# Softmax statistics settled once per node block, sums by source over 72 columns, and one load for edge features, in a two-layer graph kernel on Trainium2

## The chip, the cores and the metric

The kernel runs on one core of one Trainium2 chip. The core has five engines with instruction queues of their own, each worked off in order: PE (TensorE, matmuls; its weight loads are listed apart as PEld), DVE (VectorE), ACT (ScalarE), POOL (GpSimd) and SP (SyncE, which here only issues DMAs). They meet through semaphores alone. The metric is the device time of one execution in microseconds. Before the change it is 4238.74 us, the median of three runs (4227.38 to 4244.78).

## The reference, cut to what matters

6250 nodes with 128 features, 100,000 edges `src -> dst`, sorted by `dst`. Two graph layers, each with a residual and a layer norm. H = 8 heads of D = 16.

```python
# layer 0: attention; the softmax runs over the edges of one src
q, k, v = (x @ W.T + b for Wq, Wk, Wv)                   # each (N, H, D)
scores  = sum(q[src] * k[dst], -1) / sqrt(16) + edge_attr_8
seg_max = segment_max(scores, src)
ex      = exp(scores - seg_max[src])
weights = ex / segment_sum(ex, src)[src]
x = layernorm(x + segment_sum(v[src] * weights, dst) @ Wo.T + bo)
# layer 1: edge MLP, summed by src, then a node MLP
h   = silu(concat[x[src], x[dst], edge_attr_2] @ eW1 + eb1)
agg = segment_sum(silu(h @ eW2 + eb2), src)
x = layernorm(x + silu(concat[x, agg] @ nW1 + nb1) @ nW2 + nb2)
```

(The three projections are written as one line.) Three things are sums or maxima over all edges of one source node: `seg_max`, the sum of `ex`, and `agg`. The change touches all three.

## The kernel before

**Order of the edges.** The edges come sorted by `dst`. The kernel first puts them into order of `src`, in two regions: region 0 ("near") holds the edges with `dst` below 256, region 1 ("far") the others. A chunk is 16 tiles of 128 edges, 2048 edges; the near region has 9 chunks (`AC`), the far one 40 (`BC`). Each sorted edge is one row of the DRAM arrays `xs[r]`. Since the edges are in order of `src`, the edges of a few tiles touch a short run of node numbers. So a gather by `src` is a matmul: a one-hot matrix (`oh`, made by DVE by comparing a row of node offsets with the partition number) times a *window* of 128 consecutive rows of a table. A window serves `WT[r]` tiles: 2 near, 4 far, so 8 windows to a near chunk and 4 to a far one. The first node of each window is a number in a register, read at run time from `s0i`.

**Tables.** `q3_tab`, `k3_tab` and `v3_tab` in DRAM hold the projections of all nodes, each float32 value as a sum of three bfloat16 parts, 3 x 128 values to a row. `near_tab` in DRAM holds, for each node, the running maximum and sum (16 values) that the near edges gave. `stat_r` in SBUF (96 partitions x all nodes) takes the maxima and sums of the far edges: each of two slots for an edge run's maximum and sum has three bfloat16 parts, 96 rows.

**Stages of the traced execution.** Until about 1552 us: sorting, projections and `near_scores` (the scores and statistics of the near region). From 1552 to 2954: the *softmax stage*, the middle loop of `fast` (L909 on), over the far chunks with the near ones put between. To 3117: the messages, which the softmax stage scatters into `xmsg` by order of `dst`, are summed by `dst` (L1110). To 3172: output projection and first layer norm. From there to the end: the *edge layer* (`loads_of`, `pre_of`, `second`, `total`, `layer`; L1192 on).

**The softmax stage.** A far chunk passes these steps, each in quarters of a chunk:

- *fetch* (L511): SP loads the edge rows `st` and four windows `qw` of the q table, two buffers each.
- *turn* (L519): PE transposes columns of `st`; ACT writes node offsets to `slo_row` in DRAM and SP reads them back spread over all partitions; ACT writes the parts of the edge features to `ef_rows`.
- *score* (L578): DVE makes the one-hot `oht`; PE gathers q (`qv`, L587), DVE multiplies by k and reduces (`pr`, L590).
- *soft* (L598): scans along the edges give each run of equal `src` its maximum and its sum of exponentials.
- *stat* (L619): DVE makes `soh`, a one-hot of the last edge of each run against the 128 nodes of the window (L640); PE multiplies it with the values `v96` (L657); DVE adds the result into `stat_r` at the window's register address (L663).
- *merge* (L934): joins the statistics for the windows of this chunk. First quarter: SP loads the windows of `near_tab` into `z` and of `v3_tab` into `vw`, DVE copies the windows of `stat_r` into `tmp` (L949). Second: PE transposes `tmp` (L954) and DVE reduces the parts into `z` (L955). Third: `pooled` (L668) joins the slots into one maximum and one sum, then the reciprocal, then three bfloat16 parts `lw` (`split3`, L111 to L115). Fourth: PE spreads `lw` to the edges with the one-hot (L968), and DVE, ACT and DVE make the weights `wt` (L971 on). The same code joins the near chunks, which need all far chunks that reach their nodes.
- *message* (L990): PE gathers v (L979), DVE multiplies by `wt` (L981), and POOL scatters the rows into `xmsg`, one indirect DMA for each tile of 128 edges (L126).

**What sets the order.** A plan gives each step and quarter a due time: chunk number minus a lag of the step (fetch 6, turn 5, score 4, soft 3, stat 2.25, merge 0.9, message 0). `run` works off the plan in order of due times, and runs first what a step needs: `merge` of chunk c needs `stat` of chunk c+1, since the next chunk can still add to its last nodes; and `held` makes a step wait until an earlier chunk has given back a buffer (`score` of chunk c needs all messages of c-6). The compiler's scheduler may move instructions from there.

**The edge layer.** For each far step of four tiles, POOL gathers the rows of `b_tab` for `dst` (L118), PE transposes them into `pre` (L1217), adds the part of the edge features (`eft`, three loads per chunk, L1195 to L1197) and of the `src` nodes (`aw`), ACT applies SiLU; PE multiplies with `w2` (`po`), ACT applies SiLU to give `fe`; in `total`, DVE makes the one-hot `ohf` (128 columns), PE multiplies it in float32 with `fe` as the weights (`ps`, L1255), and DVE adds the 128 columns into `agg2` (L1259).

**Two branches.** The program has a fast branch, described here, and a general one. Tests on the data (`counts_fit`, `tell_path`) choose: no near or far count may leave an even spread by more than `SLACK`, and windows may not be wider than they are assumed to be.

Of the kernel before, what the change touches and what calls it, by code (L numbers as in the profile page):

```python
# [32 lines left out]
WT = (2, 4)  # L33
PER_BLOCK = (377.5, 1671.0)
SLACK = (512.0, 1024.0)
# [17 lines left out]
def tile_gnn(  # L53
# [28 lines left out]
    q3_tab, k3_tab, v3_tab, a3_tab = (dram.tile([NW, 3 * F], BF16, name=f"{n}3_tab") for n in "qkva")  # L82
    b_tab = dram.tile([NP, F], F32, name="b_tab")
    ka_tab = dram.tile([NW, 3 * F], BF16, name="ka_tab")
    near_tab = dram.tile([NW, 16], F32, name="near_tab")
# [183 lines left out]
    def rows_of_keys(r):  # L269
# [8 lines left out]
        if r == 0:  # L278
            nc.gpsimd.memset(none, -1.0)
            zero = ks.tile([P, 3 * F], BF16, name="zero")  # L280
            nc.gpsimd.memset(zero, 0.0)
            for tab in (k3_tab, q3_tab, v3_tab, a3_tab):
                nc.sync.dma_start(tab[NP:NW, :], zero)
            rows_of_keys.none = none
# [32 lines left out]
        over = ks.tile([p, g, P], F32, name=f"over{r}")  # L317
# [63 lines left out]
    def counts_fit():  # L381
# [6 lines left out]
        half = kp.tile([P, 2], F32, name="half")  # L388
        nc.vector.tensor_single_scalar(half[:, 1:2], iota_p, float(P // 2), ALU.is_ge)
        nc.vector.tensor_scalar(half[:, 0:1], half[:, 1:2], -1.0, 1.0, ALU.mult, ALU.add)  # L390
        sums = bank()[:, :NB]
        nc.tensor.matmul(sums[:2, :], half, cnts[1], start=True, stop=True)
        nc.vector.tensor_reduce(b[:2, 2:3], sums[:2, :], AX.X, ALU.min)
        nc.vector.tensor_single_scalar(b[:2, 2:3], b[:2, 2:3], float(4 * P), ALU.is_lt)
# [17 lines left out]
    def project_qv():  # L412
# [8 lines left out]
        nc.scalar.mul(bqv[:, 0], bqv[:, 0], D ** -0.5)  # L421
        for j0 in range(0, NB, 2):
# [12 lines left out]
            for a in range(3):  # L435
# [5 lines left out]
                for i, tab in enumerate((q3_tab, v3_tab)):  # L441
                    nc.sync.dma_start(
                        tab[j0 * P:(j0 + n) * P, a * F:(a + 1) * F].rearrange("(j p) f -> p j f", p=P),
# [36 lines left out]
    def scorer(r, sp, bank_q, bank_x, deep, dsti=None):  # L480

        c0, n = REG[r]
        nw = UC // WT[r]
# [4 lines left out]
        v96 = [sp.tile([P, UC, 96], BF16, name=f"v96_{i}", bufs=1) for i in range(2)]  # L488
# [19 lines left out]
        def window(tab, c, name, bufs):  # L508
            t = sp.tile([P, nw, 3, F], BF16, name=name, bufs=bufs)
# [14 lines left out]
        def turn(c, q):  # L524
# [32 lines left out]
            else:  # L557
# [11 lines left out]
                else:  # L569
                    nc.scalar.copy(dsti[:, c * UC:(c + 1) * UC], st[:, :, 1])  # L570
                    w["at"] = sp.tile([P, UC], I32, name="at", bufs=8)
# [7 lines left out]
        def score(c, q):  # L579
            w = works[c]  # L580
            if q == 0:
                w["oh"] = hot_of(w["row"], "oht", deep["oh"])
                w["dot"] = sp.tile([P, UC, H], F32, name="dot", bufs=8) if r else dota[:, c]
# [35 lines left out]
        def stat(c, q):  # L619
# [3 lines left out]
            v = v96[c % 2]  # L623
# [4 lines left out]
            if q == 0:  # L628
# [10 lines left out]
                w["soh"] = sp.tile([P, 4, P, 4], BF16, name="soh", bufs=deep["soh"])  # L639
# [1341 lines left out]
```

## Time and profile before

| | us |
|---|---|
| median of three runs | 4238.74 |
| lowest, highest | 4227.38, 4244.78 |
| the profiled execution | 4211.11 |
| its span (first to last instruction) | 4209.2 |
| PE busy in the span | 2643.5 (63%) |
| POOL | 2156.6 (51%) |
| PE weight loads | 2030.1 (48%) |
| DVE | 1994.6 (47%) |
| ACT | 861.8 (20%) |
| mean granted clock of TensorE | 0.713 of full speed |
| moved by DMA | 523.75 MB, mean 124 GB/s |

The span counts 65,902 instructions. Busy times of engines lie beside each other and don't add to the span. No engine is busy two thirds of it, so the whole says less than the stages do. The granted clock is between 0.5 and 0.8 in most slices until about 2900 us and 0.9 or more afterwards[...].

In the listings, a group of instructions is shown as: line, engine, operation, output <- input, sizes, number | busy us, mean ns of one | idle time of the engine just before these instructions, and what ended it ("PE x L957": a semaphore of PE from the write of `x` at line 957; "remote": a semaphore whose setter the trace doesn't name; "issue": nothing that is shown). An idle time belongs to the instruction that came after it, and all that stands behind it in the same queue has waited as well.

### The profile page before, as it was taken

The page shows a single profiled execution, that of the slowest core. Times are in us where ns is not written, and L with a number is a line of the kernel's source. Part 1 is how long each engine was busy: PE and PEld are TensorE (multiplying, and loading weights), DVE is VectorE, ACT ScalarE, POOL GpSimd, SP SyncE. Part 2 cuts the span into 40 slices and gives each one's busy share as a digit, 9 for nine tenths or more (in the row PEclk, how much of TensorE's full clock was granted, in tenths as well). Part 3 has the DMA queues.
Part 4 walks back from the last instruction along what each step waited for, and adds up shares of the span by engine and source line. Part 5 has one row for each costly group of instructions (what it writes and reads, how often), then busy time and mean ns, then how long its engine had stood idle before and what let it go on. Part 6 is the DMA issues. An engine that isn't in the chain of part 4 may idle for free. (4 is left out here: it accounts for less than half of the span.)

```text
span 4209.2 us, 65902 instructions
## 1 busy us (share of the span) xinstructions
PE 2643.5 (63%) x22552; PEld 2030.1 (48%) x22552; DVE 1994.6 (47%) x6056; ACT 861.8 (20%) x2688; POOL 2156.6 (51%) x2119
## 2 busy tenths in 40 slices
PE   6546674444444225555655666565895999898988
PEld 4444443333333224444544555454883666665655
DVE  6655335454545525555555556554892222222232
ACT  2222232122222111111111111110022222222222
POOL 3455544555555551445445444556216666666663
PEclk8555555566555556666676777576897899999999
DMA  5433545444543315434434344431754333333341
GB/s 180 130 118 103 143 138 168 139 151 132 167 130 100 110 60 142 135 109 133 122 113 127 114 120 117 138 98 50 281 197 128 109 100 98 99 110 98 101 124 46
DMA packets 492378, 523.75 MB, mean 124 GB/s; under 512 B 155562, under 2 KB 417117, under 8 KB 486912
## 3 DMA queue, kind: packets, MB, share of 16 engines
q1 hardware_dynamic: 399150, 345.09, 28.3%
q0 software_dynamic: 66048, 140.62, 10.9%
q10 hardware_dynamic: 26834, 33.73, 2.5%
q8 instruction: 180, 2.95, 0.3%
q14 instruction: 166, 1.36, 0.1%
HBM read 391.11 MB, written 128.06 MB: 123 GB/s over the span
## 5 line engine op out<-in xcount | busy, mean ns | idle before, releaser
L126 POOL DMA_INDIRECT xs<-stg,posi x784 | 803.9, 1025 | 766.1 <-ACT cs L777 337.0
L126 POOL DMA_INDIRECT xmsg<-msg,at x640 | 648.7, 1014 | 722.1 <-issue 409.4
L118 POOL DMA_INDIRECT bt<-b_tab,dsti x640 | 640.5, 1001 | 333.4 <-issue 165.4
L778 PE MATMUL base<-hi,lo 128*128 128x49 bf16 x784 | 169.6, 216 | 547.3 <-ACT cs L777 333.5
L780 PEld LDWEIGHTS <-hit 128*128 128x128 bf16 x2352 | 145.7, 116 | 546.5 <-issue 531.0
L1259 DVE TENSOR_TENSOR stat_r<-stat_r,ps 128x128 f32 x232 | 66.3, 286 | 645.7 <-PE ps L1255 223.4
L787 PE MATMUL kx<-kw,ohd 128*128 128x128 bf16 x2352 | 265.5, 284 | 97.0 <-issue 56.9
L762 DVE TENSOR_SCALAR_CACHE_REDUCE junk<-sk,meta 128x127 bf16<-128x127 int16 x784 | 298.1, 435 | 11.4 <-DMA sk<-skew 4.8
L777 ACT CAST cs<-base 128x49 bf16<-128x49 f32 x784 | 160.7, 205 | 638.3 <-remote 286.4
L787 PEld LDWEIGHTS <-ohd 128*128 128x128 bf16 x2352 | 213.9, 131 | 136.1 <-issue 129.3
L587 PEld LDWEIGHTS <-oht 128*128 128x128 bf16 x2352 | 219.3, 134 | 124.3 <-issue 63.8
L1255 PE MATMUL ps<-ohf,fe 128*128 128x128 f32 x1568 | 231.4, 292 | 52.1 <-issue 28.5
L587 PE MATMUL qv<-qw,oht 128*128 128x128 bf16 x1920 | 200.5, 287 | 97.7 <-DVE oht L576 36.3
L1240 PE MATMUL po<-w_sb,ht 128*128 128x128 f32 x1568 | 245.6, 301 | 18.7 <-issue 9.4
L1255 PEld LDWEIGHTS ps<-ohf,fe 128*128 128x128 f32 x1568 | 208.8, 205 | 62.0 <-issue 33.9
L1240 PEld LDWEIGHTS po<-w_sb,ht 128*128 128x128 f32 x1568 | 205.2, 203 | 66.8 <-issue 49.4
L979 PE MATMUL qv<-vw,oht 128*128 128x128 bf16 x1920 | 188.5, 257 | 74.2 <-DVE pr L590 34.0
L1232 ACT ACTIVATE ht<-pre 128x512 f32<-128x512 f32 x196 | 116.9, 597 | 493.1 <-PE pre L1228 199.6
L979 PEld LDWEIGHTS <-oht 128*128 128x128 bf16 x1920 | 152.9, 117 | 122.6 <-issue 92.3
L223 DVE TENSOR_TENSOR lo<-iota_e,lo_c 128x2048 bf16<-128x2048 bf16 x98 | 119.0, 1215 | 150.6 <-remote 80.2
L780 PE MATMUL look<-st_b,hit 128*128 128x49 bf16 x1568 | 164.3, 211 | 27.1 <-DVE sel L794 17.0
L1228 PE MATMUL pre<-oht,aw 128*128 128x512 bf16 (+1 forms) x696 | 171.9, 365 | 12.8 <-issue 12.4
(303 smaller groups left out, 5228.8 us busy)
## 6 DMA issues: line engine op xcount, KB each, us to landing
st<-xs SPq DMA_DIRECT2D x49, 1128.0 KB
srow<-slo_row SPq DMA_DIRECT2D x98, 512.0 KB
lob<-lob_row SPq DMA_DIRECT2D x49, 512.0 KB
drow<-dlo_row SPq DMA_DIRECT2D x49, 512.0 KB
sk<-skew SPq DMA_DIRECT2D x49, 508.0 KB
qw<-q_tab SPq DMA_DIRECT2D x232, 96.0 KB
vw<-v_tab SPq DMA_DIRECT2D x232, 96.0 KB
aw<-a_tab SPq DMA_DIRECT2D x232, 96.0 KB
```

The lines of the kernel that those rows point to most:

```text
L118: nc.gpsimd.indirect_dma_start(out=dst, out_offset=None, in_=table, in_offset=bass.IndirectOffsetOnAxis(ap=idx, axis=0))
L126: apart(nc.gpsimd.indirect_dma_start(out=table, out_offset=bass.IndirectOffsetOnAxis(ap=idx, axis=0), in_=src, in_offset=None), group)
L587: nc.tensor.matmul(qe[:, i, :], w["oh"][:, 4 * q + i, :], w["qw"][:, (4 * q + i) // WT[r], k, :], start=(k == 0), stop=(k == 2))
L762: nc.vector.tensor_scalar(junk, w["sk"][:, :, j], meta[:, c * UC + j, 0:1], 0.0, ALU.is_equal, ALU.add, accum_out=w["rank"][:, j:j + 1])
L777: nc.scalar.copy(cs, base)
L778: nc.tensor.matmul(base, lo, hi, start=False, stop=False, skip_group_check=True)
L780: nc.tensor.matmul(w["look"][:, j - 8 * h, :], w["hit"][:, j, :], tab, start=(i == 0), stop=(i == 2))
L787: nc.tensor.matmul(kx[:, i, :], w["ohd"][:, 4 * q + i, :], w["kw"][:, q, a, :], start=(a == 0), stop=(a == 2))
L979: nc.tensor.matmul(ve[:, i, :], w["oh"][:, 4 * q + i, :], w["vw"][:, (4 * q + i) // WT[r], k, :], start=(k == 0), stop=(k == 2))
L1228: nc.tensor.matmul(pre[:, i * wt:(i + 1) * wt, :], w["aw"][:, 4 // wt * q + i, k, :], w["oh"][:, 4 * q + i * wt:4 * q + (i + 1) * wt, :], ...
L1240: nc.tensor.matmul(po[:, i, :], ht[:, i, :], cw["w2"], start=False, stop=(i == 3))
L1255: nc.tensor.matmul(ps[:, i // WT[r], :], fe_[:, i, :], oh[:, i, :], start=(i % WT[r] == 0), stop=((i + 1) % WT[r] == 0))
```

## The change

1. **`merge` becomes `settle`, once for each block of nodes.** A block is 128 nodes, 49 in all. `settle(b)` transposes one block of `stat_r` straight from its place (no `tmp`), joins it with the near part, which stays in SBUF (`near_o`) instead of `near_tab`, makes maximum and reciprocal of the sum, splits them into three parts, and stores these into `v3_tab`, whose rows are widened from 3 x 128 to 3 x 144 values (`VW`). It runs when the last far chunk that can reach the block (`holds`) has been through *stat*. The step *load* (far) or *nfetch* (near) then loads windows of `v3_tab`, 144 columns to a part, that bring v and the statistics together; *weigh* spreads the last 16 columns to the edges as the fourth quarter of `merge` did.
2. **New lags and buffers.** fetch 8.5, turn 7.5, score 6.5, soft 5.5, stat 4.75, load 1.5, weigh 0.7, message 0. Eight buffers of the one-hot instead of six, twelve of `dot` and of `at` instead of eight; the holds of `turn` and `score` go to twelve and eight chunks back, and `load` needs the messages of three chunks back.
3. **72 columns for far sums by `src`.** `soh` with L657 and L663 in *stat*, and `ohf`, `ps` and their adds in the edge layer take the first 72 columns of a window instead of 128 (`WN`). `counts_fit` gets a test that this suffices.
4. **`eft` by one DMA** whose source repeats six rows three times, instead of three DMAs.
5. **Tighter `SLACK`**, 384 and 750 instead of 512 and 1024, and, in the general branch, two buffers of a tile instead of four. In the first stage, three stores put zeros into the new columns of `v3_tab`.

```diff
+WN = (P, 72)
-SLACK = (512.0, 1024.0)
+SLACK = (384.0, 750.0)
+VW = F + 16
...
+    v3_tab = dram.tile([NW, 3 * VW], BF16, name="v3_tab")
-    near_tab = dram.tile([NW, 16], F32, name="near_tab")
...
+        for a in range(3):
+            nc.sync.dma_start(v3_tab[:NP, a * VW + F:(a + 1) * VW].rearrange("(j p) f -> p j f", p=P),
+                              none.to_broadcast([P, NB, VW - F]))
...
-                w["soh"] = sp.tile([P, 4, P, 4], BF16, name="soh", bufs=deep["soh"])
+                w["soh"] = sp.tile([P, 4, wn, 4], BF16, name="soh", bufs=deep["soh"])
...
-                        to = sums_of["src"][:96, bass.ds(rg[i], P)]
-                        nc.vector.tensor_add(to, to, y[:96, (i - i0) * P:(i - i0 + 1) * P])
+                        to = sums_of["src"][:96, bass.ds(rg[i], wn)]
+                        nc.vector.tensor_add(to, to, y[:96, (i - i0) * wn:(i - i0 + 1) * wn])
...
+            def settle(b, q):
+
+                x = bank_x()[:, :96]
+                nc.tensor.transpose(x, sums_of["src"][:96, b * P:(b + 1) * P], ident[:96, :96])
+                z = sp.tile([P, 1, 3, 16], F32, name="z")
+                nc.vector.tensor_reduce(z[:, 0, 0:2].rearrange("p a v -> p (a v)"),
+                                        x.rearrange("p (k v) -> p v k", v=32), AX.X, ALU.add)
+                nc.scalar.copy(z[:, 0, 2], sums_of["near"][:, b])
+                o = sp.tile([P, 1, 16], F32, name="o")
+                pooled(o, z, sp, 1, 3)
+                nc.vector.tensor_scalar_max(o[:, :, 8:16], o[:, :, 8:16], 0.5)
+                nc.vector.reciprocal(o[:, :, 8:16], o[:, :, 8:16])
+                o3 = sp.tile([P, 3, 16], BF16, name="o3")
+                split3([o3[:, k, :] for k in range(3)], o[:, 0], sp, "orest")
+                nc.scalar.dma_start(v3_tab[b * P:(b + 1) * P, :].rearrange("p (k f) -> p k f", k=3)[:, :, F:], o3)
+
+            def weigh(r, w):
+
+                x = bank_x()[:, :256].rearrange("p (t v) -> p t v", v=16)
+                for t in range(UC):
+                    for k in range(3):
+                        nc.tensor.matmul(x[:, t, :], w["oh"][:, t, :], w["vw"][:, t // WT[r], k, F:],
+                                         start=(k == 0), stop=(k == 2))
...
+            def far_load(c, q):
+                works[c]["vw"] = s["window"](v3_tab, c, "vw1", 3, VW)
...
+            steps = {"fetch": (s["fetch"], 1, 8.5), "turn": (s["turn"], 3, 7.5), "score": (s["score"], 4, 6.5),
+                     "soft": (s["soft"], 2, 5.5), "stat": (s["stat"], 4, 4.75), "load": (far_load, 1, 1.5),
+                     "weigh": (far_weigh, 1, 0.7), "message": (far_message, 4, 0.0)}
...
+            held = {"fetch": (("score", 2),), "turn": (("score", 2), ("message", 12)),
+                    "score": (("message", 8),), "load": (("message", 3),)}
...
-                for i in range(3):
-                    nc.sync.dma_start(w["eft"][6 * i:6 * i + 6], ef_rows[r][:, c * UC * P:(c + 1) * UC * P])
+                row = ef_rows[r][0:1, :]
+                nc.sync.dma_start(w["eft"], bass.AP(tensor=row.tensor, offset=row.offset + c * UC * P,
+                                                    ap=[[0, 3], [REG[r][1] * UC * P, 6], [1, UC * P]]))
...
-                oh = el.tile([P, 4, P], F32, name="ohf", bufs=3)
+                oh = el.tile([P, 4, P], F32, name="ohf", bufs=3)[:, :, :wn]
...
-                ps = elq.tile([F, 2, P], F32, name="ps")
+                ps = elq.tile([F, 2, P], F32, name="ps")[:, :, :wn]
```

## The prediction, made before the result was known

> **What bounds the kernel now.** I read the busy times by stage first, since one share of the whole says little here (columns: stretch; its length, then busy time and count for PE, PEld, DVE, ACT, POOL; granted TensorE clock; DMA share; GB/s):
>
> ```profile
> 1552.00:2954.00 1402.00, 791.38 (x8346) 661.75 (x8346) 750.89 (x2153) 209.54 (x837) 672.12 (x660) 0.67 0.40 115
> 2954.00:3117.00 163.00, 149.12 (x1285) 147.70 (x1285) 143.52 (x321) 0.40 (x1) 24.43 (x14) 0.95 0.79 278
> ...
> 3172.00:4209.00 1037.00, 896.39 (x5229) 597.92 (x5229) 268.34 (x666) 241.68 (x414) 642.53 (x643) 0.90 0.35 100
> ```
>
> Two of these stages are touched. In the softmax stage (1552 to 2954) no engine is busy more than 56%, and the clock is 0.67: five in-order queues stand and wait for each other. In the edge layer (from 3172) PE is busy 86% at clock 0.90, and that is the bound; POOL comes next with 640 gathers of 1.001 us and 0.30 us of issue before each, 836 us.
>
> Who waits in the softmax stage is told by the groups of that stretch, with the idle time before them:
>
> ```profile
> L949 DVE COPY tmp<-stat_r 96x128 f32 x232 | 37.6, 231 | 4.4 <-issue 4.2
> ...
> L955 DVE TENSOR_REDUCE z<-x 128x128 f32<-128x384 f32 x58 | 31.4, 551 | 111.1 <-remote 76.2 <-PE x L954 12.6 <-issue 8.9
> ...
> L640 DVE TENSOR_TENSOR soh<-iota_e,last 128x2048 bf16<-128x2048 bf16 x40 | 48.6, 1216 | 0.0
> L663 DVE TENSOR_TENSOR stat_r<-stat_r,x 96x128 f32 x160 | 43.9, 274 | 24.4 <-PE x L657 15.7 <-PE qv L587 5.5 <-PE x L968 1.5
> ...
> L113 DVE TENSOR_TENSOR lr<-po,lw 128x64 f32<-128x64 f32 (+1 forms) x49 | 11.5, 234 | 72.2 <-ACT lw L111 37.1 <-issue 26.4 <-ACT sr L537 7.9
> ...
> L971 DVE TENSOR_TENSOR wt<-dot,x 128x128 f32<-128x128 f32 x40 | 11.4, 286 | 100.0 <-PE x L968 56.2 <-remote 15.8 <-PE x L1020 11.3
> ```
>
> To be seen: DVE, the engine that all others feed, stands 111 us before the merge's reduction, 72 us before its split and 100 us before the weights (29 more on the near form). Its queue is in order, so scores and messages behind these lines stand as well.
>
> **The change, part by part.** All sums are against the profiled execution: span 4209.2, its own time 4211.1 us. The median of the runs is 4238.7, 0.65% more; I add that at the end.
>
> *Merge becomes settle.* DVE's merge rows, L949, L955, the six of `pooled` (10.8, 12.9, 13.2, 12.8, 13.2, 13.3), L960 13.0, L961 18.7, L113 11.5 and L115 11.2, sum to 199.6 us. A settle does one block: one reduction of 96 elements (273 ns at L679's 96) and ten operations of 16 to 48 elements (between L529's 170 ns at 16 and L113's 234 at 64; I take 190), so 2.2 us; 49 of them are 106. DVE loses 94 us, its copies and their register loads wholly. PE loses 183 of 232 transposes at the 183 ns of L954's weight load, 33 us. SP loses 232 loads of `near_tab` (POOL and DMA gain nothing by it: 29,696 packets of 64 B at 10 ns over 16 engines are 19 us, spent again on wider rows of v and on 49 stores). ACT gains 49 copies and 49 DMA issues, some 0.55 us each, 27 us, beside 85% idle.
>
> *72 columns in `stat`.* `soh` is 1216 ns for 2048 columns; 56/128 of it, 40 times, is 21 us of DVE. L663's adds lose 56 columns at 1.03 ns (L1259's 286 ns at 128 against L1251's 682 at 512): 58 ns x160, 9 us. PE's 640 matmuls of L657 have weights of 96 columns, which need 96/128 of today's pitch of 107 ns (x16 in 1.83 us); they fall to that, not to 72/128: 17 us.
>
> *Waits.* Counted in instructions of all engines in the program as built (about 525 to a chunk), the weights of a chunk follow the merge's copies by about 200 today; after the change they follow the transposes of the last block that they need by 480 to 1250. So the chain reduce, Exp, split no longer ends in the same half chunk in which it began. I let half of the waits at L955 and L113 go (110 and 72, so 91) and a quarter of those at L971 (129, so 32): 123. Bounds: 0, if other waits take the place at once (pr at L590 stands 146 us already, for PE); 311, if all go.
>
> *How much of the work lies on the path.* DVE's 124 us and PE's 50 partly lie beside each other and beside the waits on PE. The chain of waits passes through PE and DVE by turns in this stage, so I take 60% of DVE's part, 74. Sum of gains in the stage: 197.
>
> *What the stage pays.* (a) Deeper lags: 20 quarters of scores stand before the first message where 12 did, and 27 messages behind the last one where 17 did. Ten messages are 40 scatters at 1.013+0.30 us, 53 us of POOL; the last stretch, 2826 to 2954, has POOL busy 74 of 128, so most fits in. I take 20; ends 0 and 53. (b) A new road through DRAM: settle's store waits on ACT for earlier loads of `v3_tab` to land (the table is read at register addresses, so every store is ordered behind every load), and `load` on SP waits for the store. The nearest row is `slo_row`: from the issue of its store to the issue of its load 1.4 to 9 us, median 2.7. Behind the waiting load on SP stand `qw` and `st` of a later chunk, and PE's turn waits for `st` (58.7 us today); behind the store on ACT stand the casts of `stat`. The load is followed by its first use within 26 to 100 instructions, 2 to 6 us. Today's loads of z stand as close (21 to 200) and cost DVE 12 us in all; I take 15. Ends 0 and 7 us per chunk, 280.
>
> *Edge layer, 72 columns.* Here a rule and a row weigh against the change. Both sides of a matmul are timed in this view (ns: minimum/median/maximum):
>
> ```profile
> L1255 PE MATMUL ps<-ohf,fe x1567: 269/275/582, 3199.7 to 4194.9; 128*128 128x128 f32 x196
> L1255 PEld LDWEIGHTS ps<-ohf,fe x1566: 186/192/338, 3199.7 to 4194.8; 128*128 128x128 f32 x196
> ```
>
> Each f32 matmul is two records. In order of time eight records stand in 1.06 us, a pitch of 112 ns, and every record has a weight load of its own. Matmul rule of the Trainium skill ("TensorE: Matmul & The Clock Gate", Back-to-back issue gap): streamed columns / 2.4 + 2.5. For two passes of 72 columns that is 63 ns; 160 steps x 8 x 49 is 62 us. Load rule of the same page (LDWEIGHTS): columns / 1.2, which is 107 ns for the 128 columns of `fe` whatever the moving side does, and its fast load is not given to f32. The trace sides with the second: the weight load is 192 ns for f32 in two passes, 142 for one pass (L1217), 98 for bf16 (L1228), so a pass of 128 columns is about 50 ns, two 100; and the first record of a run of eight takes 1.16 us with its load exposed against 1.06 us. With a load of about 104 ns to each record the pitch can fall only from 112 to about 107: 160 x 8 x 5 is 6 us. I take 5; ends 0 and 62. DVE's rows there shrink, but DVE is 26% busy and waits for PE.
>
> *One load for `eft`.* SP issues 98 DMAs fewer (0.33 us each), but SP stands over 500 us at this line for buffers. Only the first chunks gain, where PE stood 10 us for `eft`: 5 us.
>
> *First stage.* Three stores of zeros add 18,816 packets of 32 B; the 5120 of `skew` passed in 3.2 us, so 12 us of DMA, long before anything reads them; 13 stores of `near_tab` go. 0, ends -12 and +15, since the built order shifts a little. The longer test in `counts_fit` runs beside POOL's scatters. The tighter SLACK only moves `layer` earlier.
>
> Sum: -197+20+15-5-5 = -172; 4211-172 = 4039; times 4238.7/4211.1, **4066 us**, 4.1% less.
>
> **Rivals.** *A, nothing much comes free* (0.15): the stage's pace is set by `st` and `qw`, held in two buffers each, with a fetch that waits for a score two chunks back; this loop isn't touched. For it: the waits on `st` (99 us on ACT, 59 on PE) and SP's at L512, over 450 us. Against it: DVE's longest waits are in the merge. Gain 0 to 60: 4180 to 4240. *B, the load through DRAM takes the merge's place* (0.15): at PE's first weigh matmul of each chunk, behind SP's queue. If store, load and landing stand open by 7 us in each of 40 chunks, that is 280 against the 197 gained, and with (a) the time is 4211+280-197+20-10 = 4304, with the factor 4332. It decides from some 4.5 us per chunk on; below, the kernel is still faster. *C, all waits go and the matmul rule holds* (0.07): -74-311-62, with nothing paid, 3764 us, times the factor 3789; half way to it from the forecast is 3930. *D, the other branch is taken*, since the conditions are tighter: computed from the inputs, sorted far edges leave the even spread by at most 199 against 750, near ones by 109 against 384, and 512 edges span 43 nodes, under 72. Excluded.
>
> **Numbers.** The forecast with a gain of 60 to 260 (3980 to 4180) has 0.63, A 0.15, B 0.15, C 0.07. The range 3950 to 4245 holds forecast, A and a little of B and C: 0.8. Half a per cent, 21 us, is about what this measurement tells from no change: faster 0.77 (forecast, C and half of A), same 0.07, slower 0.16.
>
> **What would show it.** The softmax stage should end at about 1240 us length instead of 1402; DVE's waits before the weights' row and before the split should shrink, DVE's busy time there be near 627; `ps` records should keep a pitch of 107 to 112 ns with 72 columns. Wrong would be: PE idle before the weigh matmuls on DMA of `vw` (B), the same wait total under the names `pr` and `st` (A), a pitch near 63 (C).

## The result, and the profile after

The changed kernel takes 4273.65 us (median of 5 runs, 4268.63 to 4293.96), the kernel before 4238.74 (median of 5, 4221.04 to 4245.91): ratio 1.0099, 95% interval 1.0071 to 1.0126. It is 1% slower; 4066 us was forecast. The profiled execution takes 4268.63 us, its span 4266.8.

The busy times by stage, as for before (stretch; its length, then busy time and count for PE, PEld, DVE, ACT, POOL; granted clock; DMA share; GB/s), of the kernel after:

```profile
0.00:1586.50 1586.50, 766.97 (x7452) 591.17 (x7452) 781.98 (x2716) 377.97 (x1359) 791.06 (x782) 0.58 0.45 130
1586.50:2979.00 1392.50, 723.43 (x8163) 596.00 (x8163) 621.77 (x1913) 206.11 (x886) 657.33 (x659) 0.66 0.41 117
2979.00:3147.00 168.00, 147.81 (x1281) 146.34 (x1282) 145.03 (x320) 0.41 (x1) 24.88 (x14) 0.93 0.77 270
...
3203.00:4266.00 1063.00, 913.16 (x5228) 605.62 (x5228) 223.31 (x663) 241.21 (x413) 627.18 (x644) 0.87 0.34 97
```

The work that was to go is gone: in the second row DVE is busy 622 us (751 before, about 627 forecast) and PE 723 (791 before, some 741 forecast). The stage is 1393 us long all the same, against 1402. So DVE stands 770 us of it where it stood 651. The groups with idle time, of the kernel after in that stage (time in the group, mean ns | idle before it and what ended that):

```profile
L608 DVE TENSOR_TENSOR pr<-qv,st 128x512 f32<-128x512 f32 x160 | 108.1, 683 | 133.2 <-PE x L972 48.1 <-remote 42.1 <-PE qv L605 33.5
...
L972 PE MATMUL x<-vw,oht 128*128 128x16 bf16 x1920 | 89.1, 174 | 128.0 <-issue 116.7 <-DMA vw<-v_tab 11.1
...
L972 PE MATMUL x<-vw,noh 128*128 128x16 bf16 x432 | 28.8, 176 | 59.3 <-issue 44.4 <-DMA vw<-v_tab 14.8
...
L956 DVE TENSOR_REDUCE z<-x 128x32 f32<-128x96 f32 x49 | 11.5, 251 | 80.2 <-remote 74.9 <-PE x L954 2.6 <-PE tp L573 1.7
...
L115 DVE TENSOR_TENSOR orest<-o,o 128x16 f32<-128x16 f32 x49 | 8.1, 168 | 7.8 <-ACT o L113 7.8
...
L975 DVE TENSOR_TENSOR wt<-dot,x 128x128 f32<-128x128 f32 x40 | 11.5, 287 | 196.6 <-PE x L972 78.4 <-remote 39.3 <-PE qv L983 37.9
```

and the same matmuls of *weigh* in the kernel before, where they belonged to `merge`:

```profile
L968 PE MATMUL x<-lw,oht 128*128 128x16 bf16 x1920 | 77.2, 173 | 88.9 <-issue 51.2 <-ACT lw L111 24.9 <-ACT sr L537 6.0
...
L968 PE MATMUL x<-lw,noh 128*128 128x16 bf16 x432 | 19.0, 172 | 19.3 <-issue 18.3 <-ACT lw L111 0.7 <-DVE lw L115 0.2
```

The wait before the split fell from 72 to 8 us (L115 now). That before the reduction fell from 111 to 80, with 49 reductions in place of 58; its greater part is "remote" in both kernels (76 and 75 us). That before the weights doubled, from 100 to 197, and 78 us of it are put down to the *weigh* matmuls of PE (L972), as are 48 of the 133 us before the scores' product (L608). PE itself stands 128 + 59 us before these matmuls, against 89 + 19 before, and of the 187 us only 26 are put down to the load of `vw`. The rest is "issue": the engine waited for nothing that the trace shows.

Cut at the first and the last product of v and weights, and at the first instruction of each later stage, the two profiled executions compare so (us):

| | first stage | softmax: lead | messages | tail | sum by `dst` | node stage | edge layer | span |
|---|---|---|---|---|---|---|---|---|
| before | 1551.9 | 96.1 | 1298.4 | 8.4 | 161.6 | 66.6 | 1026.2 | 4209.2 |
| after | 1586.4 | 111.2 | 1252.2 | 29.4 | 167.6 | 62.4 | 1057.5 | 4266.8 |
| difference | +34.5 | +15.1 | -46.2 | +21.0 | +6.0 | -4.2 | +31.3 | +57.6 |

(Of the 57.6 us some 20 are the spread of executions: the profiled one of before, 4211.11, was faster than all five timed ones; the medians differ by 35.) By one profile each, the stretch of messages gained 46 us. Lead and tail took 36 back, and the first stage and the edge layer, for which no change and a gain of 10 us had been forecast, grew by 66.

### The profile page after: what moved, and what is told of

Read it like the earlier page. It is cut to its first block, busy times and chain, and to the rows that moved or that the text cites. A ratio compares the mean times of both kernels' runs of the same rounds, so it can differ in the third digit from the quotient of the medians.

```text
span 4266.8 us, 64192 instructions
## 1 busy us (share of the span) xinstructions
PE 2596.0 (61%) x22370; PEld 1974.6 (46%) x22370; DVE 1826.1 (43%) x5819; ACT 859.1 (20%) x2737; POOL 2127.4 (50%) x2120
## 5 line engine op out<-in xcount | busy, mean ns | idle before, releaser
L128 POOL DMA_INDIRECT xs<-stg,posi x784 | 802.9, 1024 | 800.0 <-ACT cs L793 380.7
L128 POOL DMA_INDIRECT xmsg<-msg,at x640 | 635.0, 992 | 728.9 <-DVE msg L986 351.9
L120 POOL DMA_INDIRECT bt<-b_tab,dsti x640 | 623.8, 975 | 378.3 <-issue 163.6
L1281 DVE TENSOR_TENSOR stat_r<-stat_r,ps 128x72 f32 (+1 forms) x232 | 57.1, 246 | 728.3 <-PE ps L1277 277.1
L1262 PE MATMUL po<-w_sb,ht 128*128 128x128 f32 x1568 | 255.4, 308 | 23.3 <-issue 14.6
L1277 PE MATMUL ps<-ohf,fe 128*128 128x72 f32 (+1 forms) x1568 | 224.6, 289 | 60.8 <-issue 45.5
L605 PEld LDWEIGHTS <-oht 128*128 128x128 bf16 x2352 | 216.6, 133 | 96.8 <-issue 69.1
L605 PE MATMUL qv<-qw,oht 128*128 128x128 bf16 x1920 | 211.6, 289 | 71.5 <-issue 48.6
L983 PE MATMUL qv<-vw,oht 128*128 128x128 bf16 x1920 | 174.8, 242 | 56.0 <-issue 36.2
L1131 PE MATMUL ps<-ohd,mt 128*128 128x128 f32 x1280 | 147.7, 279 | 56.9 <-DMA mt<-xmsg 53.7
```

What stands on the lines that cost most here:

```text
L120: nc.gpsimd.indirect_dma_start(out=dst, out_offset=None, in_=table, in_offset=bass.IndirectOffsetOnAxis(ap=idx, axis=0))
L128: apart(nc.gpsimd.indirect_dma_start(out=table, out_offset=bass.IndirectOffsetOnAxis(ap=idx, axis=0), in_=src, in_offset=None), group)
L605: nc.tensor.matmul(qe[:, i, :], w["oh"][:, 4 * q + i, :], w["qw"][:, (4 * q + i) // WT[r], k, :], start=(k == 0), stop=(k == 2))
L983: nc.tensor.matmul(ve[:, i, :], w["oh"][:, 4 * q + i, :], w["vw"][:, (4 * q + i) // WT[r], k, :F], start=(k == 0), stop=(k == 2))
L1262: nc.tensor.matmul(po[:, i, :], ht[:, i, :], cw["w2"], start=False, stop=(i == 3))
L1277: nc.tensor.matmul(ps[:, i // WT[r], :], fe_[:, i, :], oh[:, i, :], start=(i % WT[r] == 0), stop=((i + 1) % WT[r] == 0))
```

## The experiments

**Two sorts of chips.** The executions fell on several chips, each beside executions of the kernel before on the same one. On four chips before took 3243 to 3249 us (medians of 19 to 39 runs); on the chip of the result 4239, and on one more 4299 (11 runs). Same program, same data. I call them quick and slow chips below. Times can't be compared across the two sorts; what differs between them is the key to this case. A second profile of the kernel before, on a quick chip, shows where the 1000 us are:

> The kernel before, a second profile, to see how far the stages move from one execution to the next: I expect each stage within 15 us of the first profile (1552, 1402, 163, 55, 1037), and the stretches in which PE, DVE, ACT and SP advance by one instruction in 0.7 us to sum to 60 to 120 us again.

```profile
0.00:1114.00 1114.00, 711.70 (x7449) 561.90 (x7451) 777.83 (x2713) 371.41 (x1359) 801.23 (x763) 0.66 0.62 184
1114.00:2176.00 1062.00, 705.92 (x8346) 605.53 (x8346) 745.01 (x2155) 211.67 (x837) 691.38 (x678) 0.75 0.53 153
2176.00:2339.00 163.00, 149.87 (x1287) 148.44 (x1288) 142.13 (x320) 0.41 (x1) 24.07 (x14) 0.94 0.80 278
...
2395.00:3241.00 846.00, 805.10 (x5132) 558.84 (x5229) 271.02 (x665) 248.72 (x412) 625.57 (x643) 0.98 0.43 122
```

It took 3243.6 us, far outside the 15 us per stage that I had expected, and the hold-ups in steps of 0.7 us, of which a piece is shown further below, are not in it. Against the rows of the first profile, the sum by `dst` (163 us, third row) is the same. The first stage lost 438 us of 1552, the softmax stage 340 of 1402, the edge layer 191 of 1037, with nearly the same busy times of POOL and DVE. These three are the stages in which POOL issues indirect DMAs (784 + 640 scatters, 640 gathers). The three waits that the prediction took for those of `merge` (before reduction, split and weights) are 31, 21 and 35 + 7 us in this profile, 95 in all, where the first one had 312.

**The parts of the change, on quick chips.** *Settle alone*: the changed kernel with

```diff
-WN = (P, 72)
+WN = (P, P)
...
-                nc.sync.dma_start(w["eft"], bass.AP(tensor=row.tensor, offset=row.offset + c * UC * P,
-                                                    ap=[[0, 3], [REG[r][1] * UC * P, 6], [1, UC * P]]))
+                for i in range(3):
+                    nc.sync.dma_start(w["eft"][6 * i:6 * i + 6], ef_rows[r][:, c * UC * P:(c + 1) * UC * P])
```

> The changed kernel with 128 columns again in stat and in the edge layer and with three loads of eft: settle, the wide rows of v and the new lags alone. Theory 1 (the softmax stage gained nothing because of settle and the road around it): the softmax stage stays near the 1392 us of the changed kernel, at 1390 to 1430, and the first stage stays some 30 us longer than before. Theory 2 (72 columns or the single load cost what settle gains): the softmax stage falls to 1300 or less. For the edge layer: if 72 columns or the eft load made it 26 us longer, it is back at 1037 here; if it varies from execution to execution, it can be anywhere from 1030 to 1065.

> The changed kernel with 128 columns everywhere and three loads of eft, once more. Where before takes about 4240 to 4300 us: Theory 1 (the edits of the edge layer lengthened it): edge layer 1025 to 1045 here; Theory 2 (a reason outside it): 1055 or more. First stage 20 us or more longer than that of the kernels with the old first stage, by either. Softmax stage 5 to 30 us shorter than before by either. Where before takes about 3250 us: 3220 to 3230 in all, as in the first run of it.

Ratio to before 0.993 (0.9914 to 0.9947), and on a second quick chip 0.9919 (0.9903 to 0.9936). Softmax stage 1021 and 1020 us against 1062: on these chips settle, with its lags, gains 41 us there. The first stage takes 1127 and 1129, against 1111 to 1119 in six profiles with the old first stage. Neither theory's size was right, since both had the slow chip's stages in mind.

*The edge layer's edits*, each alone in the kernel before, then together, then the changed kernel without them:

```diff
-                oh = el.tile([P, 4, P], F32, name="ohf", bufs=3)
+                oh = el.tile([P, 4, P], F32, name="ohf", bufs=3)[:, :, :wn]
...
-                ps = elq.tile([F, 2, P], F32, name="ps")
+                ps = elq.tile([F, 2, P], F32, name="ps")[:, :, :wn]
```

> The kernel before with 72 columns in the edge layer alone (ohf, ps and their adds). Theory 1 (fewer streamed columns leave the matmul bound by its weight load and the granted clock falls a little): edge layer 1050 to 1065 us at a clock of 0.85 to 0.88, the whole run 10 to 25 us slower. Theory 2 (as predicted, load-bound and otherwise neutral): edge layer 1027 to 1037 us, whole run within 10 us of before. Theory 3 (the matmul rule): 975 us.

> The kernel before with the single load of eft alone. Theory 1 (as predicted): edge layer 2 to 8 us shorter than 1037, nothing elsewhere. Theory 2 (one DMA of 18 rows lands later than three of 6, and PE waits for it at the first steps of each chunk): edge layer 10 to 30 us longer, with PE idle before L1224 on DMA of eft.

> The kernel before with the two edits of the edge layer alone: 72 columns in ohf, ps and their adds, and the single load of eft. On a chip where before takes about 4240 to 4300 us: Theory 1 (these two edits lengthened the edge layer, which took 1058 to 1089 us in the changed kernel against 1026 to 1038): 1060 us or more here, clock there at 0.88 or less. Theory 2 (the edge layer is longer for a reason outside it): 1025 to 1040. Where before takes about 3250 us: 835 to 840 by either.

> The kernel before with the two edits of the edge layer, once more, since the first run of it fell on a chip where before takes 3243 us and showed 837 us by either theory. Where before takes about 4240 to 4300 us: Theory 1 (these edits lengthened the edge layer from 1026 to 1038 to 1058 to 1089): 1055 or more. Theory 2 (a reason outside them): 1025 to 1045.

> The kernel before with the two edits of the edge layer, for the third time, to see it on a chip where before takes 4240 to 4300 us. There: Theory 1 (these edits lengthen the edge layer): 1055 us or more. Theory 2 (a reason outside them): 1025 to 1045. Where before takes about 3245 us it is 837 again and tells nothing new.

> The changed kernel with the edge layer of before (128 columns, three loads of eft). Where before takes 4240 to 4300 us: Theory 1: edge layer 1025 to 1045 and the whole run 25 to 50 us faster than the changed kernel; Theory 2: 1055 or more. Where before takes about 3245 us: within 5 us of the changed kernel, 3212 to 3222.

All six fell on quick chips. 72 columns alone: 0.9979 (0.9967 to 0.999), 7 us; the single load alone: 0.9997 (0.9985 to 1.001); both: 0.9997 (0.9987 to 1.0007), 0.9993 (0.9982 to 1.0004) and 0.9996 (0.9982 to 1.001). The edge layer of these kernels takes 832 to 839 us, 837 before. So the 7 us of the first run are not seen in that layer (835 us, 2 less), and three runs with both edits on other chips show 1 to 2 us in all: a gain from 72 columns there is not shown. The changed kernel with the old edge layer: 0.9893 (0.9875 to 0.9912), edge layer 847, so what lengthens that layer by 6 to 10 us on quick chips lies outside these edits. Why it is 31 us longer on the chip of the result, none of these runs could say.

*The whole change on a quick chip*:

> The changed kernel as it is, so far timed only on chips where the kernel before takes 4240 to 4300 us. Where before takes about 3245 us: Theory 1 (there POOL's scatters bound the stretch of messages): first stage 1125 to 1130, stretch of messages 850 to 857, edge layer 838 to 848, whole run 3205 to 3225, 0.7 to 1.2% faster than before. Theory 2 (72 columns bring more): 3200 or less. Where before takes about 4240 to 4300: 1% slower, for the third time.

0.9897 (0.988 to 0.9913): here the change makes the kernel 1.0% **faster**, in the middle of what the first theory gave. Its stages: first 1135.5 (1125 to 1130 expected), lead 130.7, messages 846.9, tail 35.2, edge layer 843.0. For what bounds it, two groups of this run in the stretch of messages:

```profile
L128 POOL DMA_INDIRECT xmsg<-msg,at x614 | 617.4, 1006 | 311.0 <-issue 145.9 <-DVE msg L986 90.3 <-DVE dot L612 22.0
...
L986 DVE TENSOR_TENSOR msg<-qv,wt 128x512 f32<-128x512 f32 x160 | 108.5, 682 | 114.1 <-DMA xmsg<-msg,at 112.0 <-PE x L972 1.6 <-PE vt L653 0.3
```

614 scatters of 1.006 us and some 0.30 us of issue before each are 802 of the 847 us; POOL's pauses over 0.6 us sum to 39, where they were 100 in before on a quick chip. DVE waits 112 us before it writes a message, and what ends the wait is the landing of an earlier scatter, which gives the buffer back. In before there was no such wait (0.6 us in the profile on a quick chip). So here the merge's wait was not simply removed: the stage ran into the pace of POOL's scatters.

**Without the scatters.** In both kernels the 640 indirect scatters were replaced by 160 plain stores on the same queue; the order by `dst` is left out:

```diff
-                for i in range(4):
-                    scatter(xmsg, w["at"][:, 4 * q + i:4 * q + i + 1], ms[:, i, :], "xmsg")
+                t0 = (AC + c) * UC + 4 * q
+                apart(nc.gpsimd.dma_start(xmsg.rearrange("(p t) f -> p t f", p=P)[:, t0:t0 + 4, :], ms), "xmsg")
```

> The changed kernel as it is. In the runs so far the kernel before took 3248 us where it had taken 4239 us for the result; where before takes about 3250 us: Theory 1 (POOL's 640 scatters at 1.33 us, 851 us, bound the stretch from the first to the last message, so that nothing beyond settle and lags can shorten it): softmax stage 1015 to 1030 us as in the run of settle alone, first to last product of v and weights 850 to 860 us, whole run 3210 to 3235. Theory 2 (72 columns in stat still bring DVE and PE time): softmax stage 985 to 1000. Where before takes about 4240 us: 4260 to 4290 again.

> The changed kernel with the 640 indirect scatters of the messages replaced by 160 plain stores on the same queue of POOL, four tiles each; the order by dst of the messages is left out. Theory 1 (scatters set the pace of the softmax stage, by POOL's time or by what they do to the other engines): the stage falls by 80 us or more against the changed kernel where before takes about 3250 us, to some 900 to 940, and by 250 us or more where before takes about 4240 us. Theory 2 (the loop of st, qw and score sets the pace): the stage stays within 30 us.

> The kernel before with the same plain stores; the order by dst of the messages is left out. Theory 1: the gain that the trace of before promised shows once the scatters are gone, so the softmax stage of this kernel is 80 us or more longer than that of the changed kernel with plain stores. Theory 2: the two stages differ by 40 us or less, as with the scatters.

These fell on the second slow chip, where before takes 4298.84 us. The changed kernel: 1.0109 (1.0069 to 1.0149), the result once more. With plain stores: 0.8917 (0.8872 to 0.8961) for the changed kernel and 0.9024 (0.8985 to 0.9062) for before. The stages (us; the chip of the result for the first row):

| | first stage | lead | messages | tail | softmax in all | edge layer |
|---|---|---|---|---|---|---|
| before | 1551.9 | 96.1 | 1298.4 | 8.4 | 1402.9 | 1026.2 |
| before, plain stores | 1589.2 | 92.9 | 914.6 | 4.8 | 1012.4 | 1034.8 |
| after, again | 1619.5 | 111.1 | 1272.9 | 27.2 | 1411.2 | 1083.7 |
| after, plain stores | 1613.5 | 109.7 | 791.5 | 4.7 | 905.9 | 1089.4 |

Theory 1 held. The changed kernel's softmax stage lost 505 us with the scatters, and with plain stores it is shorter than any quick chip made it with them. Without scatters, the change (settle, lags and 72 columns in *stat*) shortens the stretch of messages by 123 us and the stage by 106; with them, the first profiles differ by 10. That is where the gain of this stage went. Of the whole run only 42 us are left without scatters (3830.60 against 3872.44), since the first stage and the edge layer are longer by 24 and 55 us there. Whether it is the scatters' issue on POOL, their number, or the single rows that they write all over `xmsg`, these runs don't separate.

They also show what the waits were. The kernel before with plain stores, its softmax stage (columns as above) and the three waits in it:

```profile
1589.20:2601.60 1012.40, 696.09 (x8346) 597.01 (x8346) 743.80 (x2155) 208.97 (x838) 112.14 (x180) 0.77 0.53 159
...
L955 DVE TENSOR_REDUCE z<-x 128x128 f32<-128x384 f32 x58 | 31.2, 549 | 30.3 <-PE x L954 29.7
L971 DVE TENSOR_TENSOR wt<-dot,x 128x128 f32<-128x128 f32 x40 | 11.5, 288 | 33.6 <-PE x L968 28.4 <-PE x L657 2.9 <-PE qv L979 1.8
L113 DVE TENSOR_TENSOR lr<-po,lw 128x64 f32<-128x64 f32 (+1 forms) x49 | 11.4, 232 | 19.8 <-ACT lw L111 19.7
L971 DVE TENSOR_TENSOR wt<-dota,x 128x128 f32<-128x128 f32 x9 | 2.6, 288 | 6.7 <-PE x L968 6.7
```

and the changed kernel with plain stores:

```profile
1613.50:2519.40 905.90, 619.94 (x8163) 531.52 (x8163) 615.02 (x1913) 205.10 (x886) 110.67 (x178) 0.78 0.60 180
...
L975 DVE TENSOR_TENSOR wt<-dot,x 128x128 f32<-128x128 f32 x40 | 11.5, 287 | 63.0 <-PE x L972 57.0 <-PE qv L605 4.8 <-PE vt L667 1.1
L956 DVE TENSOR_REDUCE z<-x 128x32 f32<-128x96 f32 x49 | 11.4, 248 | 9.6 <-PE x L954 9.5
L115 DVE TENSOR_TENSOR orest<-o,o 128x16 f32<-128x16 f32 x49 | 8.1, 168 | 6.2 <-ACT o L113 6.0
L975 DVE TENSOR_TENSOR wt<-dota,x 128x128 f32<-128x128 f32 x9 | 2.6, 288 | 39.0 <-PE x L972 39.0
```

The 312 us of waits in the first profile of before are 90 on a slow chip without scatters, near the 95 of a quick chip: the rest was not `merge`'s own. Nor does the change lower these 90; afterwards they are 118. What it gains without scatters is work: DVE is busy 129 us less, the stage is 106 us shorter, and DVE stands 291 us of it where it stood 269.

What a scatter does to others on a slow chip is seen on SP's register moves, which wait for nothing. The kernel before on the chip of the result, with scatters (duration in ns: minimum/median/maximum, then first and last start):

```profile
L945 SPq MOVE vw<-v_tab x232: 2/29/1391, 1614.0 to 2888.3; - x116
```

the changed kernel on the second slow chip, with scatters:

```profile
L530 SPq MOVE vw<-v_tab x160: 2/29/1382, 1725.4 to 2952.8; - x160
```

the same with plain stores, same chip:

```profile
L530 SPq MOVE vw<-v_tab x160: 29/29/38, 1717.9 to 2497.5; - x160
```

the changed kernel on a quick chip, with scatters:

```profile
L530 SPq MOVE vw<-v_tab x160: 29/29/38, 1261.0 to 2054.9; - x160
```

and moves in the edge layer of the run with plain stores, where POOL's gathers stayed:

```profile
L1226 SPq MOVE aw<-a_tab x232: 2/29/1396, 2750.5 to 3778.6; - x116
```

These moves take 29 ns, never over 38, on the quick chip or without scatters; among scatters on a slow chip single ones take up to 1391, in both kernels, and among gathers up to 1396. PE is held up likewise. A piece of the timeline of the kernel after, from the profile of the result (start, duration, engine and instruction, idle time before it):

```profile
2374.69 0.10 PEld L972 LDWEIGHTS <-oht 128*128 128x128 bf16 x1 [1.98 <-issue]
2375.39 0.17 PE L972 MATMUL x<-vw,oht 128*128 128x16 bf16 x1 [1.92 <-issue]
2375.62 0.96 POOL L128 DMA_INDIRECT xmsg<-msg,at  x1 [0.30 <-issue]
2376.09 0.10 PEld L972 LDWEIGHTS <-oht 128*128 128x128 bf16 x1 [1.29 <-issue]
2376.88 0.96 POOL L128 DMA_INDIRECT xmsg<-msg,at  x1 [0.30 <-issue]
2377.49 0.22 PE L972 MATMUL x<-vw,oht 128*128 128x16 bf16 x2 [1.93 <-issue]
...
2378.89 0.10 PEld L972 LDWEIGHTS <-oht 128*128 128x128 bf16 x1 [1.28 <-issue]
2379.59 0.17 PE L972 MATMUL x<-vw,oht 128*128 128x16 bf16 x1 [1.88 <-issue]
...
2380.67 0.49 PE L972 MATMUL x<-vw,oht 128*128 128x16 bf16 x11
```

While POOL scatters, PE issues one or two records of *weigh* and then none for 0.7 or 1.4 us, waiting for nothing that is shown. This goes on for some 3 us after the last scatter of the row, begun at 2376.88, though POOL begins no other before 2388; then PE runs eleven matmuls in 0.49 us. DVE's weights of that chunk wait for these matmuls, and such waits are among the 197 us before L975.

**The first stage.** Three suspects among the passing edits, each alone in the kernel before. *Wide rows of v with the three stores of zeros* (v is loaded in three pieces of 256 B, so its softmax stage, 1458 us, is no guide):

> The kernel before with the rows of v of 3 x 144 values and the three stores of zeros, which nothing else uses; merge loads v in three pieces of 256 B. Only the first stage is of interest. Theory 1 (zeros and wider rows lengthen the first stage): it is 10 us or more longer than before, as in the run of settle alone (1127 against 1114), or 25 us or more where before takes about 4240 us. Theory 2 (it varies by the order in which the program was scheduled): within 6 us of before.

On the slow chip 1594 us, 5 more than the 1589 of the old first stage there and 19 to 25 less than the changed kernel. The whole run is slower, 1.011 (1.0067 to 1.0153); the loads in pieces are the likely cause, but before was not profiled on that chip. *One buffer of `v96` in the near scoring*, which the change makes to find room for `near_o`:

```diff
-        v96 = [sp.tile([P, UC, 96], BF16, name=f"v96_{i}", bufs=1) for i in range(2)]
+        v96 = [sp.tile([P, UC, 96], BF16, name=f"v96_{i}", bufs=1) for i in range(deep["soh"])]
```

> The kernel before with one buffer of v96 instead of two in the scoring of the near edges, which the change does in passing. Theory 1 (this is what lengthens the first stage): the first stage is longer than before by 20 us or more where before takes about 4240 to 4300 us, by 8 us or more where it takes about 3250. Theory 2 (the rest of the first stage's edits, among them the longer test of the counts): within 6 us of before.

The first stage takes 1110 on a quick chip, the run 0.9986 (0.9977 to 0.9995) of before: not this, there. *The longer test of the counts* (`counts_fit` as changed, in the kernel before):

> The kernel before with the longer test of the counts for a band of 72 nodes in place of the test for 64, and nothing else. Theory 1 (this test, on DVE and PE in the middle of the first stage, is what lengthens that stage): first stage 1122 or more where before takes about 3245 us (1110 to 1119 without it, 1127 to 1128 in the runs of settle), or 1610 or more where before takes about 4290. Theory 2 (the rest of the first stage's edits): 1110 to 1119, or 1585 to 1600.

The first stage takes 1124, and the run is slower by 1.0027 (1.0016 to 1.0038), 9 us. So the test is a good part of the 13 us by which the first stage is longer on quick chips (mean of four profiles against mean of six), though kernels with the old first stage differ by 9 us there among themselves. What it costs on a slow chip was not measured, and no run tells what makes the first stage 24 to 35 us longer there.

**The lags.** The deep lags lengthen the lead; can it be had back?

```diff
-            steps = {"fetch": (s["fetch"], 1, 8.5), "turn": (s["turn"], 3, 7.5), "score": (s["score"], 4, 6.5),
-                     "soft": (s["soft"], 2, 5.5), "stat": (s["stat"], 4, 4.75), "load": (far_load, 1, 1.5),
+            steps = {"fetch": (s["fetch"], 1, 6.5), "turn": (s["turn"], 3, 5.5), "score": (s["score"], 4, 4.5),
+                     "soft": (s["soft"], 2, 3.75), "stat": (s["stat"], 4, 3.25), "load": (far_load, 1, 1.25),
```

> The changed kernel with two buffers of v96 in the near scoring (room for it from one buffer of cap, fw and sm there) and with shorter lags: fetch 6.5, turn 5.5, score 4.5, soft 3.75, stat 3.25, load 1.25. Theory 1 (the lags cost lead-in at the start of the softmax stage, the single v96 costs the first stage): lead to the first message back from 111 to 93 to 100 us (from 131 to 112 to 118 where before takes about 3250), first stage 20 us shorter than that of the changed kernel (10 us where before takes 3250), whole run 25 to 45 us faster than the changed kernel. Theory 2 (the deep lags are needed to cover the road through DRAM): the stretch of messages grows by 20 us or more and eats it.

```diff
-                return c - steps[name][2] * min(1.0, 0.4 + 0.06 * c) + q / 4
+                return c - steps[name][2] * min(1.0, 0.2 + 0.06 * c) + q / 4
```

> The changed kernel with the lags of the first chunks cut: the factor of a lag starts at 0.2 instead of 0.4 and reaches 1 at chunk 14 instead of 10. Theory 1 (the lead before the first message is paid in full, since POOL's scatters bound all that follows): lead 131 falls to 110 to 120, the stretch of messages stays at 847 to 857, whole run 8 to 20 us faster than the changed kernel where before takes about 3245 us. Theory 2 (the early chunks then wait for settle): the stretch of messages grows by what the lead loses.

The first of the two also changes buffers of the near scoring, which bear on the first stage (1123 us). Both fell on quick chips. The lead fell as expected, to 116.5 and 113.3 us from 130.7, but the stretch of messages grew from 847 to 890 and 895, and the runs ended level with before: 1.0005 (0.9995 to 1.0016) and 0.9999 (0.9982 to 1.0017). Theory 2 held twice, and in the second run the stretch grew by 48 us where the lead lost 17. With settle, the lead is the price of the stretch; whether the lags alone, with the old merge, would bring the same stretch was not tried. No version clearly beat the changed kernel on a quick chip. On slow chips only two with all of their scatters were timed, the changed kernel and the wide rows, and both were slower than before.

## Why the prediction was wrong, step by step

- **Work removed**: right. DVE 622 us busy in the stage (627 said), PE 723 (741 said). One row in it was read wrongly: PE's matmuls of *stat* were to be held by their 96 columns of weights, and to lose 25% of their pitch. By the starts of these matmuls it fell from 116 to 70 ns (medians of the two first profiles), nearly as the streamed columns, 128 to 72.
- **Waits and the share on the path**: this is the step that failed. The 197 us of gain in the stage were 123 us of waits, half of 182 and a quarter of 129, and 74 us of work, 60% of DVE's. It took all of these waits for the latency of `merge`. Without scatters they are 90 us on a slow chip, and the change raises them to 118: nothing came from waits. From work came more than was said, but only without scatters: the stage is 106 us shorter for 129 us of DVE's work removed. With scatters the stretch shortened by 46 us and the stage by 10. POOL, busy 672 of 1402 us, was not considered as a bound. On quick chips it is the pace of POOL's scatters that ends the gain (62 us of 908 in the stretch, mean of eight profiles before); on slow ones, what the scatters do to the other engines.
- **Cost (a), lags**: 20 us said; lead and tail together took 36 here, some 14 on quick chips. The number of scores ahead of the first message was right (20 and 12 in the traces), its price was mis-sized.
- **Cost (b), the road through DRAM**: 15 us said; 26 us of PE's idle time before *weigh* ended with `vw`, in 6 waits. Rival B named the right place, PE before the weigh matmuls, for another reason, and its 7 us per chunk for the road did not come. Without scatters PE waits 59 us for `vw` there, in 44 waits.
- **Rival A** came nearest: DVE's standing time did not fall, it came back under other names and grew from 651 to 771 us. Its loop of `st` and `qw` was the wrong one, as the plain stores show; its lower end, no gain, still missed a loss.
- **Edge layer, rule against row**: the row was right. The two lines of the kernel after:

```profile
L1277 PEld LDWEIGHTS ps<-ohf,fe x1568: 186/192/338, 3238.4 to 4253.9; 128*128 128x128 f32 x196
L1277 PE MATMUL ps<-ohf,fe x1568: 223/275/489, 3238.4 to 4253.9; 128*128 128x72 f32 x160, 128*128 128x128 f32 x36
```

  Each weight load still takes 192 ns with 72 columns streamed. Within a run of eight the mean pitch is 106 ns on a quick chip against 112 with 128 columns; the load bound gave 107, the matmul rule 63. (The section of the Trainium skill that was cited for that rule, Back-to-back issue gap in "TensorE: Matmul & The Clock Gate", gives it for a matmul by itself, and says that it counts too little where each matmul has a weight load.) The single load of `eft`, for which 5 us were said, gained nothing that its interval (5 us less to 3 more) tells from zero. What was missed is that this layer would grow on slow chips. It does so in all three profiles of the changed kernel there, 1058, 1084 and 1089 us against 1026, 1035 and 1038 with the old layer, and the granted clock in it goes along, 0.87, 0.85 and 0.86 against 0.90, 0.91 and 0.91. Whether the lower clock is the cause, and what lowers it, is open.
- **First stage**: 0 was said, with -12 to +15; it was +34.5 here, +24 to +30 between kernels on the second slow chip, +13 on quick ones. The zeros, which I priced, cost little. The longer test, which I waved through as "beside POOL's scatters", costs about 9 us (5 to 12) on a quick chip, so POOL's scatters don't cover it there.

The sign followed from the sum of these: 46 us gained, 36 of lead and tail, and 66 in the two stages around. Against the forecast, -172 us in the span where +58 were measured, 152 us are missing in the softmax stage (-162 said, -10 found), 41 in the edge layer and 35 in the first stage.

Three things are left open. What lengthens the first stage on slow chips; what lengthens the edge layer there, since the runs with and without its edits fell on quick ones; and how scatters hold up the other engines of a slow chip. POOL's scatters take no longer there, 1.01 and 0.99 us with 0.30 us before each; but its pauses over 0.6 us in the stretch of messages sum to 468 us before and 461 after, against 100 and 39 on quick chips.

## What to carry to other kernels

When every engine of a stage is idle a good part of the time, look first for instructions that wait for nothing and still come late (a register move that takes 1391 ns where 29 is usual, as in the trace of before; long "issue" before matmuls): while those are there, work taken off a waiting engine is not time taken off the stage, and an idle time before an instruction need not be the latency of what it waits for. Taking the suspected disturber out showed it here: 312 us of waits became 90. Then set the new stage length against each engine's own floor, count times pitch: 640 scatters at 1.31 us were 60% of the stage before and would have been 68% of the stage that was forecast, which bounds what any gain elsewhere can bring. And price each passing edit, the guard and the smaller buffer too, in the stage where it stands: here two stages around the changed one decided the sign.

## What the runs showed of the hardware

Chips differ: one program took 3243 to 3249 us on four and 4239 and 4299 on two, and a change that was 1.0% faster on the first sort was 1.0 and 1.1% slower on the second. The difference lies in the stages with indirect DMAs from POOL, and in the softmax stage it goes with them: with plain stores from the same queue, 0.56 us of issue each, the changed kernel's stage took 906 us on a slow chip, where its scatters had made it 1411. How the scatters do it, and what the slow chips have in common, was not found.
